# A four-layer graph network on one Trainium2 core: 36 sorted blocks instead of 32, 21 gathered blocks instead of 20, the sort's result through DRAM, gathers sent further ahead

## The chip, the cores and the metric

The kernel runs on one core of one Trainium2 chip. The metric is the time of the whole program on that core in microseconds (us), taken on the device. A profile comes from one execution of its own, which the hardware profiler recorded. The engines are called PE (matrix multiplication; PEld is its loading of weights), DVE (vectors), ACT (scalars and activations), POOL (general purpose, and here the engine that sends all DMAs with computed addresses) and SP (which sends plain DMAs).

## What is computed

N = 6250 nodes with C = 256 features, E = 100000 directed edges, four layers. The edges arrive sorted by destination, with random sources.

```python
def agg(h):
    return jax.ops.segment_sum(h[src], dst, num_segments=N)
x0 = x
x = jnp.maximum(_layernorm(x, axis=-1), 0.0)
for l in range(3):
    h = x + agg(x)
    h = jax.nn.relu(h @ W1s[l] + b1s[l])
    h = jax.nn.relu(h @ W2s[l] + b2s[l])
    x = h @ W3s[l] + b3s[l]
h = x + agg(x)
h = jax.nn.relu(h @ cW1 + cb1)
h = jax.nn.relu(h @ cW2 + cb2)          # cW2: 256 x 64, cW3: 64 x 256
return x0 + h @ cW3 + cb3
```

## The kernel before

**Blocks.** The nodes lie in NT = 49 blocks of 128 rows. The first 32 places (NS) are "s" blocks: all nodes of 32 row blocks are sorted by their number of incoming edges, and the s blocks hold them in that order, those with the fewest edges first. The other 17 (U) are "u" blocks, whose rows stay where they were. What a layer has computed for an s block is scattered row by row to the table in DRAM (`place_rows`: an indirect DMA that POOL sends, lines L598 and L600); u blocks are stored by SP as plain rows.

**Two ways to sum over the edges.** For most destination blocks PE does it. The features of all 49 row blocks lie on the chip in `XY`, as a high and a low part; for a *panel* of three or four destination blocks PE multiplies them with a matrix `a` of edge counts, 49 steps j of four matmuls each, 196 in a panel (`product`, L2087), summing into `agg`. A panel of four is 512 columns wide, one of three 384. The count matrices are stored as bytes in DRAM; SP loads them (`at<-mat`), ACT turns them into floats (L2052). For the s blocks with the fewest edges the sum is gathered instead (class `ByNode`): for the c-th edge of each of 128 nodes one indirect DMA, sent by POOL (L1761), brings 128 rows of the table; two at a time they are added by DVE into `sums` (L1798). A block whose nodes have at most 14 edges costs 14 such gathers. When a block is summed, PE turns it (`pt`, L1825), and it goes through the layer's dense part (`mlp`).

**A layer.** The panels come one after the other on PE; each closed panel goes through the dense part (L1567, L1570, L1666, L1671; in the last layer L1581, L1624, L1650) some steps later, in the midst of the next panel. The gathers run beside the panels. The last gathered block of a layer goes through a hastened form (`rush`, L1498 to L1533), and the last panel's own dense part follows at the start of the next layer. A layer's first gather may start only when every row of the table is written, since it may read any of them; PE may start the next layer at once with the u blocks, which stand first in `ORDER`, because they are kept on the chip. The s blocks come back from the table two at a time (`pairs_back`, tile `turned`), three such loads in flight.

**Layer 0** has more to do. The counts are not given: PE builds the matrices from one-hot vectors that DVE writes (L1234; PE L1288, ACT L1296), a little ahead of the panel that reads them. The sort by degree, its permutation of the nodes' words (generator `listed`, L1854 to L1870: one-hots on DVE, 32 small matmuls on PE) and the lists of addresses for the gathers also lie here: for each gathered block POOL fetches its nodes' edges (L1886, 20 requests ahead of the first gather), and 13 further requests bring the edges of the s blocks that PE sums.

**The order of the work.** Nothing is scheduled by a tool: the program is written step by step of PE's panels (`tick`), and every other engine's instruction is put into its queue at a step. `ByNode.flow` sends as many gathers at each step as a model of PE's time allows (`clock`, divided by `pace`, plus a lag from `LAGS`); `after` makes a gather wait until PE has come to the step. Eight tiles of two gathers each hold the rows on their way (`FIRST_TILES`, `MORE_TILES`). POOL works through its queue in order: a scatter that waits for its rows holds the gathers behind it.

Of the kernel before, what the change touches and what calls it, by code (L numbers as in the profile page):

```python
# [9 lines left out]
F32 = mybir.dt.float32  # L10
# [9 lines left out]
P = 128  # L20
# [400 lines left out]
def sorted_edges(  # L421
# [69 lines left out]
    NS = 32  # L491
# [3 lines left out]
    seq = [("u", b) for b in range(NS, NT - 3)] + [("s", b) for b in range(NS - 1, NS - 13, -1)] + [  # L495
        ("u", b) for b in range(NT - 3, NT)] + [("s", NS - 13)]
    early = [(0, 3)] + [(b, 4) for b in range(3, 23, 4)] + [(23, 3), (26, 3)]
    wide = [(b, 4) for b in range(0, 20, 4)] + [(20, 3), (23, 3), (26, 3)]
# [3 lines left out]
    nodes_of = [[(16, 4), (12, 4), (8, 4), (4, 4), (1, 3), (0, 1)]] * NLAYER + [  # L502
        [(15, 4), (11, 4), (7, 4), (3, 4), (1, 2), (0, 1)]]
# [34 lines left out]
    goal = const.tile([P, 2, NS], BF16, name="goal")  # L538
    V = 6
    what = const.tile([P, NS, V], BF16, name="what")  # L540
# [9 lines left out]
    tables = [dram.tile([N + PAD, C], F32, name=f"table{l}") for l in range(NLAYER + 1)]  # L550
    owns = [dram.tile([P * max(KS), C], F32, name=f"own{l}") for l in range(NLAYER + 1)]
# [43 lines left out]
    def place_rows(key, ap, b, sb, **kw):  # L595

        if placing[0]:
            nc.gpsimd.memset(mark, 0.0)  # L598
        placing[0] = True
        got = nc.gpsimd.indirect_dma_start(  # L600
            out=ap, out_offset=bass.IndirectOffsetOnAxis(ap=ids[:, b:b + 1], axis=0),
            in_=sb, in_offset=None, **kw)
        wrote(key, got, True)
# [291 lines left out]
    def ranking(pool):  # L895
# [5 lines left out]
        nc.gpsimd.tensor_copy(what[:, :, 0], place[:, 0:1].to_broadcast([P, NS]))  # L901
        nc.gpsimd.tensor_copy(what[:, :, 1], colf[:, :NS])
# [46 lines left out]
        nc.scalar.copy(what[:, :, 2], ps[:, :NS])  # L949
# [14 lines left out]
        at = pool.tile([P, NS], I32, name="at_i", bufs=1)  # L964
        nc.vector.tensor_tensor(at, ps[:, :NS], begins, OP.add)
# [35 lines left out]
        nc.vector.tensor_copy(goal, where)  # L1001
        bits = pool.tile([P, 3, NS], I32, name="bits", bufs=1)
        nc.vector.tensor_scalar(bits[:, 0], at, P - 1, None, op0=OP.bitwise_and)
        nc.vector.tensor_scalar(bits[:, 1], at, 7, None, op0=OP.arith_shift_right)
        nc.vector.tensor_scalar(bits[:, 2], at, 14, None, op0=OP.arith_shift_right)
# [1216 lines left out]
```

## Time and profile before

| | |
|---|---|
| median of 3 runs | 1986.4 us (1983.7 to 1999.28) |
| the profiled execution | 1992.96 us, its span 1991.1 us, so 1.9 us lie around the span |
| granted PE clock in it, mean | 0.966 |
| PE busy | 1853.7 us, 93% of the span |
| POOL busy | 1338.7 us, 67% |
| ACT / DVE busy | 1210.6 us, 61% / 915.1 us, 46% |
| start to layer 0's first panel | 153.3 us |
| layers 0, 1, 2, 3, by the first matmul of each | 522.6, 439.6, 438.1, 437.5 us |

The profile gives each engine's busy time, but a PE that is busy may run at a lower granted clock, and POOL's time between two requests, in which it prepares the next, isn't counted as busy. Rows of a group say: line, engine, operation, written tile <- read tiles, count | busy us, mean ns of one | idle us ahead of them, and which event ended that idle time. Rows of a timeline say: start, length, engine, line, operation, and in brackets the idle time ahead and what ended it.

### The profile page before, as it was taken

What the parts mean: (1) busy time and instruction counts of PE and PEld (TensorE: products, weight loads), DVE (VectorE), ACT (ScalarE), POOL (GpSimd) and SP (SyncE); (2) the same over time, 40 slices, a digit from 0 to 9 for tenths busy, and PEclk for the clock granted to TensorE, in tenths of its full rate; (3) what the DMA queues carried; (4) which work ended last, traced back from release to release, by engine and by line L of the source; (5) the groups of instructions that cost most, each with busy time, mean ns of one, the idle gap of its engine ahead of it and who ended that gap; (6) DMA issues with size and microseconds to landing.
All of it is one profiled execution on the core that took longest, in us unless ns stands there. A gap on an engine that the chain in (4) does not pass through costs nothing. (4 is left out here: it accounts for less than half of the span.)

```text
span 1991.1 us, 29317 instructions
## 1 busy us (share of the span) xinstructions
PE 1853.7 (93%) x9334; PEld 1483.0 (74%) x9334; DVE 915.1 (46%) x1915; ACT 1210.6 (61%) x2370; POOL 1338.7 (67%) x1496
## 2 busy tenths in 40 slices
PE   4868999999999899999999899999999899999896
PEld 3746666776788777777898777777898777777774
DVE  6789788676564243332333343333334353332232
ACT  3766666676666476566566376565665576665562
POOL 2521777777777566676777566677777567777775
PEclk9878999999999999999999899999999999999898
DMA  5523665666556485565566575555566676665663
GB/s 176 176 97 115 182 195 168 203 215 217 168 174 211 157 281 181 154 199 172 178 189 212 166 232 164 163 174 165 165 195 197 193 223 208 173 180 149 147 181 81
DMA packets 247119, 357.22 MB, mean 179 GB/s; under 512 B 33368, under 2 KB 201880, under 8 KB 246666
## 3 DMA queue, kind: packets, MB, share of 16 engines
q0 software_dynamic: 65584, 167.88, 29.2%
q1 hardware_dynamic: 179184, 184.72, 28.6%
q10 hardware_dynamic: 2186, 2.65, 0.4%
q8 instruction: 75, 1.23, 0.2%
q14 instruction: 90, 0.74, 0.1%
HBM read 289.20 MB, written 70.92 MB: 181 GB/s over the span
## 5 line engine op out<-in xcount | busy, mean ns | idle before, releaser
L2087 PE MATMUL agg<-a,XY 128*128 128x512 f32 (+1 forms) x6272 | 1471.4, 387 | 14.5 <-ACT a L2052 11.0
L1761 POOL DMA_INDIRECT rows<-table,idxN x1119 | 1076.6, 962 | 422.0 <-PE agg L2087 207.1
L2087 PEld LDWEIGHTS agg<-a,XY 128*128 128x128 f32 x6272 | 1150.1, 191 | 212.5 <-ACT a L2052 21.2
L2052 ACT CAST a<-at 128x512 fp32r<-128x512 uint8 (+1 forms) x1561 | 876.7, 585 | 328.6 <-PE agg L2087 317.9
L1798 DVE TENSOR_TENSOR sums<-sums,rows 128x512 f32<-128x512 f32 x471 | 328.5, 697 | 650.2 <-DMA rows<-table,idxN 627.0
L1296 ACT CAST at<-bp 128x392 uint16<-128x392 f32 x213 | 102.8, 488 | 119.9 <-PE bp L1288 115.8
L1567 PE MATMUL ps<-h,w 128*128 128x512 f32 (+1 forms) x312 | 132.5, 568 | 4.1 <-DVE zz L1671 3.1
L600 POOL DMA_INDIRECT table<-zz,ids x96 | 96.5, 1005 | 55.8 <-DVE zz L1533 23.0
L1666 PE MATMUL ps<-w,h 128*128 128x256 f32 x576 | 133.2, 384 | 0.0
L1666 PEld LDWEIGHTS ps<-w,h 128*128 128x128 f32 x576 | 110.8, 194 | 15.1
L1288 PE MATMUL bp<-hi,lo 128*128 128x98 bf16 x964 | 88.6, 219 | 32.5 <-DVE lo L1234 25.2
L1288 PEld LDWEIGHTS <-lo 128*128 128x128 bf16 x964 | 54.3, 103 | 86.1 <-DVE lo L1234 42.4
L1234 DVE TENSOR_TENSOR lo<-lanes,pairs 128x512 bf16<-128x512 bf16 x240 | 99.3, 423 | 31.4 <-PE bp L1288 30.1
L1567 PEld LDWEIGHTS ps<-h,w 128*128 128x128 f32 x312 | 60.0, 194 | 56.7 <-issue 38.4
L1671 DVE TENSOR_TENSOR zz<-ps,w 128x512 f32<-128x512 f32 x78 | 49.6, 647 | 103.2 <-PE ps L1666 102.1
L1570 ACT ACTIVATE h<-ps,bias 128x512 f32<-128x512 f32 (+1 forms) x78 | 49.8, 656 | 55.8 <-PE ps L1567 55.8
L1833 ACT ACTIVATE h<-pt,bias 128x256 f32<-128x256 f32 (+1 forms) x80 | 32.7, 460 | 83.3 <-PE pt L1825 83.3
L1234 DVE TENSOR_TENSOR hi<-hi,pairs 128x784 bf16<-128x784 bf16 x120 | 69.3, 578 | 4.2
L1234 DVE TENSOR_TENSOR hi<-cols,pairs 128x784 bf16<-128x784 bf16 x120 | 67.2, 560 | 0.6 <-ACT pairs L1222 0.6
L1886 POOL DMA_INDIRECT lane<-padded,at x20 | 20.3, 1016 | 65.5 <-PE bp L1288 59.7
L1392 DVE TENSOR_TENSOR XY<-turned,XY 128x512 fp32r<-128x512 f32 x48 | 32.7, 694 | 67.4 <-ACT XY L1391 67.3
L600 POOL DMA_INDIRECT out_dram<-zz,ids x32 | 50.8, 1588 | 15.2 <-issue 7.1
(261 smaller groups left out, 958.5 us busy)
## 6 DMA issues: line engine op xcount, KB each, us to landing
at<-mat SPq DMA_DIRECT2D x112, 448.0 KB
mat<-at SPq DMA_DIRECT2D x30, 784.0 KB
at<-mat SPq DMA_DIRECT2D x62, 336.0 KB
rows<-table,idxN POOLq DMA_INDIRECT x1119
turned<-table SPq DMA_DIRECT2D x48, 256.0 KB
at<-mat SPq DMA_DIRECT2D x50, 224.0 KB
at<-mat SPq DMA_DIRECT2D x84, 112.0 KB
own<-zz SPq DMA_DIRECT2D x59, 128.0 KB
```

What stands on the lines that cost most here:

```text
L600: got = nc.gpsimd.indirect_dma_start(out=ap, out_offset=bass.IndirectOffsetOnAxis(ap=ids[:, b:b + 1], axis=0), in_=sb, in_offset=None, **kw)
L1234: nc.vector.tensor_tensor(o, values, which[:, :, None, :].to_broadcast(shape), op)
L1288: mm = nc.tensor.matmul(bp[:, m * HW:(m + 1) * HW], lo[:, m, :], hi[:, m, :], start=(i == 0), stop=(i == len(sets) - 1))
L1296: nc.scalar.copy(o, v)
L1567: mm = nc.tensor.matmul(ps[:, :w], weights[l][0][:, c, i * P:(i + 1) * P], h1[:, c, :w], start=(c == 0), stop=(c == KC - 1))
L1570: later(soon, lambda: nc.scalar.activation(h2[0][:, i, :w], ps[:, :w], AF.Relu, bias=b2[l][:, i:i + 1]))
L1666: mm = nc.tensor.matmul(o, h2[0][:, c, nodes], w3[:, c, :], start=(c == 0), stop=(c == KC - 1))
L1671: later(soon, lambda: nc.vector.tensor_tensor(z[:, :m, :], v, w3[:, KC:, :].to_broadcast([P, m, C]), OP.add))
L1761: got = nc.gpsimd.indirect_dma_start(out=t[:, c % 2, :], out_offset=None, in_=tables[self.l][:, :], in_offset=bass.IndirectOffsetOnAxis(ap ...
L1798: nc.vector.tensor_tensor(sums, sums, rows.rearrange("p h c -> p (h c)"), OP.add)
L2052: nc.scalar.copy(o, v)
L2087: mm = nc.tensor.matmul(agg[c][:, :w], XY[:, j, o:o + P], a[:, :w], start=(i == 0 and half == 0), stop=(i == NT - 1 and half == 1))
```

## The change

All of it is on the same program; line numbers in the changed program are some 2 to 40 higher (a gather is L1791, a scatter L602, PE's panels L2116).

1. **Blocks.** NS 32 becomes 36, so 13 u blocks are left. 21 blocks are gathered in layers 0, 1, 2 (20 before), 19 in the last (as before). Counted over the lists, layer 0 sends 312 gathers (304), layers 1 and 2 send 291 each (284), the last 257 (267). The group that comes last is now the highest of the gathered blocks, block 20 (18 in the last layer), instead of block 0.
2. **Panels.** 28 blocks are summed by PE in layers 0 to 2 (29 before), 30 in the last (30). Layer 0: 3, 3, 3, 3, 4, 4, 4, 4 blocks (3, 4, 4, 4, 4, 4, 3, 3). Layers 1 and 2: seven panels of 4 (five of 4, three of 3). The last layer's widths stay.
3. **Sort.** The 32 matmuls and the one-hots of the permutation go. POOL scatters four words for each of 36 x 128 nodes to a table `ranks` in DRAM (36 requests), and one DMA reads it back as `got`. Of the list fetches, 8 come ahead of the first gather instead of 20; 13 more, and 17 requests for s blocks' edges instead of 13, lie among the gathers.
4. **Sending ahead.** Up to 3 (layer 0) or 5 gathers more may be sent at a step, if a tile is free. In the model, `SLOW` is 1.15 instead of 1, the lag of layers 1 to 3 is 11 instead of 12, and `AHEAD_OF` 9 instead of 4.
5. **Held scatters.** In layers 1 and 2 the scatters of the group (4, 4) and of the panel next to the last (s blocks 20 on) are put behind the layer's last gather in POOL's queue; their rows wait in tiles `xt`.
6. Small things: the u rows' own copies are loaded six blocks to a panel, the hastened chain's steps stand one step apart instead of two, `pairs_back` is called when the whole layer is stored.

```diff
-    NS = 32
+    NS = 36
-    early = [(0, 3)] + [(b, 4) for b in range(3, 23, 4)] + [(23, 3), (26, 3)]
-    wide = [(b, 4) for b in range(0, 20, 4)] + [(20, 3), (23, 3), (26, 3)]
+    early = [(b, 3) for b in range(0, 12, 3)] + [(b, 4) for b in range(12, 28, 4)]
+    wide = [(b, 4) for b in range(0, 28, 4)]
     final = [(b, 4) for b in range(4, 24, 4)] + [(24, 3), (27, 3), (0, 4)]
-    nodes_of = [[(16, 4), (12, 4), (8, 4), (4, 4), (1, 3), (0, 1)]] * NLAYER + [
-        [(15, 4), (11, 4), (7, 4), (3, 4), (1, 2), (0, 1)]]
+    nodes_of = [[(16, 4), (12, 4), (8, 4), (4, 4), (0, 4), (20, 1)]] * NLAYER + [
+        [(14, 4), (10, 4), (6, 4), (2, 4), (0, 2), (18, 1)]]
...
+        for g in range(NS):
+            place_rows("ranks", ranks[:, :], g, what[:, g, :], goal)
...
+            got = pool.tile([P, NS, 4], I32, name="got")
+            back = nc.gpsimd.dma_start(out=got, in_=ranks.rearrange("(p b) v -> p b v", p=P))
+            waits(back, [name for name, _ in written["ranks"]], "each node's words lie alone")
...
+            fetch_list(0)
+            fetch_list(1)
+            for _ in range(9):
+                yield
+            nc.vector.tensor_copy(ids, got[:, :, 0])
...
+            make_list(0)
...
-                if beside is not None and (p or i % 2):
+                if beside is not None and i % (3 if p else 2) == 0:
                     next(lists, None)
...
+        def holds(l, blocks):
+            if l in (0, NLAYER):
+                return False
+            b0, n = panels[l][-2]
+            return blocks in ([("s", nodes_of[l][-3][0] + i) for i in range(nodes_of[l][-3][1])],
+                              seq[b0:b0 + n])
...
-                    self.send(int((clock[0] - self.first + self.lag) / self.pace) + 1)
+                    self.send(int((clock[0] - self.first + self.lag) / self.pace) + 1 +
+                              MORE_AHEAD[self.l > 0], True)
...
+                        if early and taken[0] == FIRST_TILES + (late is not None) * MORE_TILES:
+                            return
...
+                    if self.sent == len(self.order):
+                        while held_rows:
+                            put(*held_rows.pop(0))
...
-        LAGS, CLOSE, AHEAD_OF, NEAREST, CLOSING = (9.0, 12.0), 2.0, 4.0, 5.0, 40.0
+        LAGS, CLOSE, AHEAD_OF, NEAREST, CLOSING = (9.0, 11.0), 2.0, 9.0, 5.0, 40.0
+        MORE_AHEAD = (3, 5)
```

On POOL, between the preparation of the features (`XY`) and the first gather of layer 0, the program before has this (the tile `lane` takes the fetched edges):

```order
L1093 TENSOR_TENSOR XY<-zs,XY 128x256
L1886 DMA lane<-padded,at 128x17 x4
L1886 DMA lane<-padded,at 128x16 x4
L1886 DMA lane<-padded,at 128x15 x4
L1886 DMA lane<-padded,at 128x14 x4
L1886 DMA lane<-padded,at 128x12 x3
L1886 DMA lane<-padded,at 128x10
L1761 DMA rows<-table_87,idxN 128x256 x16
```

and the changed program has, behind 34 more pairs of a scatter to `ranks` and a memset, this (the tile `run` takes the edges of gathered blocks, `edges` those of blocks that PE sums):

```order
L600 MEMSET mark 1x4
L602 DMA ranks<-what,goal 4608x4
L1887 DMA got<-ranks 128x144
L1893 DMA run<-padded,got 128x17 x4
L1893 DMA run<-padded,got 128x16 x4
L1791 DMA rows<-table_87,idxN 128x256 x13
L1893 DMA edges<-padded,got 128x63
L1791 DMA rows<-table_87,idxN 128x256
L1893 DMA run<-padded,got 128x14 x4
```

So 12 list fetches have moved behind the first gathers, and 36 scatters and a read stand ahead of them.

At the end of layer 1, POOL's queue before ends with a group's last four gathers and four scatters, the last of them that of the hastened block (table_88 is the layer's input, table_89 its result):

```order
L1761 DMA rows<-table_88,idxN 128x256 x4
L600 DMA table_89<-zz,ids 6378x256
L598 MEMSET mark 1x4
L600 DMA table_89<-zz,ids 6378x256
L598 MEMSET mark 1x4
L600 DMA table_89<-zz,ids 6378x256
L598 MEMSET mark 1x4
L600 DMA table_89<-zz,ids 6378x256
L1761 DMA rows<-table_89,idxN 128x256 x106
```

In the changed program 48 gathers stand ahead of 13 scatters, eight of them from `xt`; this piece begins with the last of the eight:

```order
L602 DMA table_89<-xt,ids 6378x256
L600 MEMSET mark 1x4
L602 DMA table_89<-zz,ids 6378x256
L600 MEMSET mark 1x4
L602 DMA table_89<-zz,ids 6378x256
L600 MEMSET mark 1x4
L602 DMA table_89<-zz,ids 6378x256
L600 MEMSET mark 1x4
L602 DMA table_89<-zz,ids 6378x256
L600 MEMSET mark 1x4
L602 DMA table_89<-zz,ids 6378x256
L1791 DMA rows<-table_89,idxN 128x256 x117
```

On PE at that place, the program before turns the last gathered block one step (four matmuls) after the next layer has begun; the rows begin with the dense part of a gathered group, and L1567 is the last panel's own:

```order
L1666 MATMUL ps<-w_8249,h_11874 128x256 x6
L2087 MATMUL agg<-a,XY 128x384 x12
L1567 MATMUL ps<-h_11943,w_8247 128x384 x4
L2087 MATMUL agg<-a,XY 128x512 x4
L1498 MATMUL pt<-ident,u 128x128 x2
L2087 MATMUL agg<-a,XY 128x512 x4
L1514 MATMUL ps<-h1s,w_8247 128x128 x4
L1666 MATMUL ps<-w_8249,h_11948 128x256 x6
L2087 MATMUL agg<-a,XY 128x512 x4
L1527 MATMUL ps<-w_8249,h1s 128x256 x2
L2087 MATMUL agg<-a,XY 128x512 x184
```

and the changed program turns it two steps ahead of the end of the layer's last panel:

```order
L1691 MATMUL ps<-w_8304,h_11581 128x256 x8
L2116 MATMUL agg<-a,XY 128x512 x20
L1522 MATMUL pt<-ident,u 128x128 x2
L2116 MATMUL agg<-a,XY 128x512 x4
L1538 MATMUL ps<-h1s,w_8302 128x128 x4
L2116 MATMUL agg<-a,XY 128x512 x4
L1551 MATMUL ps<-w_8304,h1s 128x256 x2
L1592 MATMUL ps<-h_11692,w_8302 128x512 x4
L2116 MATMUL agg<-a,XY 128x512 x4
L1691 MATMUL ps<-w_8304,h_11697 128x256 x8
L2116 MATMUL agg<-a,XY 128x512 x176
```

So the block's chain (turn, second and third product) has moved from the start of the next layer to the end of this one, and the last panel's own dense part, four blocks wide now, is what is left behind the boundary.

More of the change, by code (lines that the diff above doesn't have):

```diff
@@ L1360, in step @@
             g["steps"].pop(0)()
-            free[0] = now[0] + (2 if g["hurry"] else 4)
+            free[0] = now[0] + (1 if g["hurry"] else 4)
             if g["steps"]:
@@ L1489, in store @@
             if stored[l] == NT:
+                assert placed[l] == NS and not held_rows
+                pairs_back(l)
                 layers[l + 1].begin()
@@ L1726, in ready @@
                     return False
-                if self.l == NLAYER and now[0] >= ends[self.l] - 2:
+                if now[0] >= ends[self.l] - (2 if self.l == NLAYER else 0):
                     return True
@@ L1950, in listed @@
                     yield
+                if j % 3 == 0:
+                    fetch_list(2 + j // 3)
+                    if j and 1 + j // 3 < len(lists):
+                        make_list(1 + j // 3)
                 if j < HELD:
@@ L2065, in product @@
                 ask_first()
-            if l == 1 and p < NS // 4:
-                for b in range(4 * p, 4 * p + 4, 2):
-                    later(12 + 6 * (b % 4), lambda b=b: own_rows(b, b + 2))
+            if l == 1:
+                for i, b in enumerate(range(6 * p, min(6 * p + 6, NS), 2)):
+                    later(10 + 12 * i, lambda b=b: own_rows(b, b + 2))
             agg = [ps_a.tile([P, W], F32, name="agg") for _ in range(KC)]
```

173 lines of the change are left out of this document (81 added, 92 removed).

## The prediction

> **What bounds the kernel now.** First the page: busy shares, then the span in slices.
>
> ```profile
> span 1991.1 us, 29317 instructions
> PE 1853.7 (93%) x9334; PEld 1483.0 (74%) x9334; DVE 915.1 (46%) x1915; ACT 1210.6 (61%) x2370; POOL 1338.7 (67%) x1496
> PE   4868999999999899999999899999999899999896
> POOL 2521777777777566676777566677777567777775
> ```
>
> PE is full nearly everywhere; POOL never reaches 8 tenths, and looks far from a bound. That reading needs the stages: start, layers 0 to 3.
>
> ```profile
> 0.00:153.30 153.30, 102.30 (x664) 78.60 (x665) 110.94 (x310) 87.27 (x208) 54.28 (x104) 0.85 0.47 151
> 153.30:675.90 522.60, 495.86 (x3000) 377.15 (x3001) 358.85 (x866) 341.02 (x727) 365.28 (x388) 0.98 0.59 184
> 675.90:1115.50 439.60, 428.00 (x1918) 352.11 (x1917) 149.06 (x248) 266.15 (x493) 304.81 (x338) 0.99 0.61 191
> 1115.50:1553.60 438.10, 428.54 (x1919) 353.95 (x1917) 149.69 (x248) 263.75 (x488) 303.46 (x340) 0.98 0.59 180
> 1553.60:1991.10 437.50, 399.03 (x1840) 321.18 (x1838) 146.60 (x244) 252.47 (x458) 310.83 (x329) 0.95 0.60 171
> ```
>
> Columns: window; its length; busy us of PE, PEld, DVE, ACT, POOL; granted clock, DMA share, GB/s. PE idles 26.7 us in layer 0, 11.6 and 9.6 in layers 1 and 2, 38.5 in the last with its tail. Removing matmuls can give about what PE is busy with, provided that POOL delivers as early. So POOL's own groups, in a stretch late in layer 1 and one late in the last layer:
>
> ```profile
> L1761 POOL DMA_INDIRECT rows<-table,idxN x102 | 97.2, 953 | 32.2 <-PE agg L2087 13.9 <-issue 10.4 <-PE ps L1666 1.8
> L600 POOL DMA_INDIRECT table<-zz,ids x20 | 19.8, 992 | 4.9 <-issue 3.7 <-DVE sums L1794 0.6 <-DVE sums L1798 0.5
> L598 POOL MEMSET mark<- 1x4 f32 x14 | 1.3, 92 | 0.0
> ...
> L1761 POOL DMA_INDIRECT rows<-table,idxN x161 | 153.1, 951 | 49.1 <-PE agg L2087 20.4 <-issue 20.4 <-DVE sums L1798 3.3
> L600 POOL DMA_INDIRECT out_dram<-zz,ids x21 | 33.4, 1592 | 5.9 <-issue 4.7 <-DVE sums L1798 0.6 <-DMA rows<-table,idxN 0.6
> ```
>
> The first stretch is 960 to 1114 us: busy 118.3, idle 37.1, together all of it. The idle time is 0.3 us per request, whoever is named as its releaser: a gather occupies POOL (97.2+32.2)/102 = 1.27 us, a scatter with its memset 1.30 to 1.33; in the last layer 1.256 and (33.4+5.9)/21 = 1.87, with its memset's 8.6/21 on top at most 2.28. **POOL is saturated there at "7 tenths".** So each layer is a cycle: a gather stream, the last block's chain, the table's last write, the next layer's first gather. Its joints, in the timeline:
>
> ```profile
> 673.22 0.95 POOL L1761 DMA_INDIRECT rows<-table,ids  x1 [0.30 <-PE agg L2087]
> 680.75 0.44 PE L1498 MATMUL pt<-ident,u 128*128 128x128 f32 x2 [3.45 <-DVE u L1816]
> 693.39 0.98 POOL L1761 DMA_INDIRECT rows<-table,idxN  x1 [2.24 <-PE agg L2087]
> 1113.82 0.95 POOL L1761 DMA_INDIRECT rows<-table,idxN  x1 [0.30 <-issue]
> 1119.71 0.69 PE L1498 MATMUL pt<-ident,u 128*128 128x128 f32 x2 [2.79 <-DVE u L1812]
> 1129.94 1.17 POOL L600 DMA_INDIRECT table<-zz,ids  x1 [11.19 <-DVE zz L1533]
> 1133.54 0.97 POOL L1761 DMA_INDIRECT rows<-table,idxN  x1 [2.42 <-PE agg L2087]
> ```
>
> From one layer's `pt` to the next is 1119.71 - 680.75 = 438.96 us, first gather to last 420.4. At saturated prices 284 gathers and 28 scatters take 284x1.27 + 28x1.32 = 398. So POOL had some 22 us of slack, held back early in the layer by the pacing, and PE (428 busy) is the tighter of the two by a little. I work with both clocks and take the later.
>
> **Layers 1 and 2.** What PE saves: a panel of four and a panel of three, their 196 matmuls alone:
>
> ```profile
> 1176.60:1229.70 53.10, 46.91 (x196) 36.79 (x197) 1.00 0.57 172
> 1012.50:1052.80 40.30, 35.94 (x199) 34.65 (x198) 1.00 0.68 209
> ```
>
> Three panels of 3 become two of 4: 3x35.94 - 2x46.91 = 14.0 less; the whole panels, with what else PE does in them, give 3x40.3 - 2x53.1 = 14.7, of which one block's dense part only moves to another place. I take 12: PE's 428 becomes 416. The boundary's idle 10 us shrinks to about 4, since `pt` now stands ahead of the panel's end and its wait is filled by the panel: PE's clock says 420.
>
> POOL's clock: 291x1.26 + 23 scatters among them x1.33 = 397 for the stream. Behind it come last gather to `pt`, 5.9 (1113.82 to 1119.71), and `pt` to first gather, 13.8 before. The moved chain is the same; the 13 scatters behind the last gather take 13x1.33 = 17.3, beside the 16.1 from last gather to the hastened scatter (1129.94). I put `pt` to first gather at 18, since the 4-wide last panel stores its u rows later. 397 + 5.9 + 18 = 421, and 4 for tiles that aren't free: **425**. POOL is the later one. 438.96 - 425 = 14 a layer, with a range of 5 (the slack stays) to 20 (PE's clock and less): **-27 for both**.
>
> That the eight held scatters cost nothing rests on the chain of the last block: POOL stood idle for 11.19 us before the scatter at 1129.94. Without that cover each would cost 1.33, 10.6 in all. Held behind them are that chain's own scatter and the next layer's first gather, nothing else. In exchange the gathers in front of them come 10.6 us earlier.
>
> **The sort.** What goes on DVE and PE, and POOL's start:
>
> ```profile
> L1863 DVE TENSOR_TENSOR moved<-block,what 128x768 bf16<-128x768 bf16 x8 | 7.7, 958 | 0.3
> L1854 DVE TENSOR_TENSOR lane<-lanes,goal 128x512 bf16<-128x512 bf16 x8 | 5.5, 683 | 0.0
> L1858 DVE TENSOR_TENSOR block<-lanes,goal 128x128 bf16<-128x128 bf16 x8 | 2.3, 282 | 0.0
> 123.87 3.81 POOL L1093 TENSOR_TENSOR XY<-zs,XY 128x512 fp32r<-128x512 f32 x3 [1.71 <-ACT XY L1088]
> 187.40 0.98 POOL L1886 DMA_INDIRECT lane<-padded,at  x1 [59.72 <-PE bp L1288]
> L1886 POOL DMA_INDIRECT lane<-padded,at x20 | 20.3, 1016 | 65.5 <-PE bp L1288 59.7 <-issue 5.2 <-DVE lo L1234 0.3
> 213.81 0.94 POOL L1761 DMA_INDIRECT rows<-table,idxN  x1 [0.30 <-issue]
> 155.00:205.00 50.00, 43.35 (x330) 36.14 (x328) 47.23 (x110) 32.11 (x78) 13.64 (x14) 0.95 0.36 112
> ```
>
> DVE loses 15.5 us of work in a stretch in which it is full (47.23 of 50). POOL is free at 127.7 and stood 59.7 us waiting. In that hole go 36 scatters. No 16-byte scatter is in the trace. The nearest rows are L600's (992 plus gap and memset, 1.33) and the fetches (1.016 + 0.3); ends: 1.2 and 2.3 (the last layer's scatter). I take 1.33: 48 us, to 175. Landing 2.4 (from the wait ahead of 1133.54), the read 1 plus some 3 (last gather to `pt`, 5.9, less the sum): **the first list fetch at about 181.5** against 187.4. DVE's copy of `got` stands at step 20 of panel 0, some 173 to 177 at 1.0 to 1.2 us a step (59.1 us for its 49 before, a panel of 3 in both programs), and the first list's arithmetic seven steps on needs edges that land near 188; so DVE and then PE stall some 10 us there in all, which eats most of the 15.5.
>
> The Trainium skill, "DMA: Bandwidth & Descriptors", section "SWDGE vs HWDGE vs iDMA", says that POOL writes its requests' descriptors into on-chip memory from which DVE's two-port mode locks it out. That speaks against 36 scatters in DVE's fullest stretch. In the row above, fetches beside a full DVE took 1016 ns against 953 for gathers beside a light one, so by the trace the rule is worth 6%, some 3 us of the 48, which changes the sum by less than its range. Taken at its worst, with POOL shut out for as long as DVE is busy, the scatters would not be done before 200 and the page's rule would make the sum about nothing.
>
> **Layer 0** has 30 list and edge fetches more among its gathers (8 ahead). Its stream in the trace and its price late in the layer (560 to 674 us):
>
> ```profile
> L1761 POOL DMA_INDIRECT rows<-table,idxN x67 | 65.2, 973 | 22.2 <-issue 11.3 <-PE agg L2087 5.3 <-DVE lo L1234 1.2
> ```
>
> A gather takes 87.4/67 = 1.305. Before: 33 fetches, 304 gathers and 28 scatters from 187.40 to 674.17 are 486.8 for 365 requests, 1.334 each. After: 38 + 312 + 31 = 381 requests. At 1.334 they end at 181.5 + 508 = 690; at saturated prices (38x1.32 + 312x1.305 + 31x1.33 = 498) at 680; at layer 1's 1.26 a gather at 665. PE saves 11 us of a panel and part of its 26.7 idle and would reach that place at 650 to 663. POOL is the later: I take 680 against 674.2, and count **+7** with the longer chain behind it; range -9 to +15.
>
> **Last layer.** Its joints:
>
> ```profile
> 1557.88 0.44 PE L1498 MATMUL pt<-ident,u 128*128 128x128 f32 x2 [2.93 <-DVE u L1812]
> 1570.58 0.97 POOL L1761 DMA_INDIRECT rows<-table,idxN  x1 [2.26 <-PE agg L2087]
> 1960.92 0.95 POOL L1761 DMA_INDIRECT rows<-table,idxN  x1 [0.30 <-issue]
> ```
>
> Same panels, 257 gathers (-10) and 29 scatters among them (25 before): -12.6 + 4x1.87 = -5; but the first gather comes at `pt` + 18, against 12.7 here. The stream had slack in its first part, which sending five ahead uses. The tail of 30 us behind the last gather has the same instructions. **-5**, range -12 to +3.
>
> **Sum:** +7 - 27 - 5 = -25. The profiled execution took 1992.96, so it would take 1968; the median of the runs lies 6.6 lower, at 1986.4, and from that I forecast **1961**. The DMA engines (0.59 to 0.61 busy) carry 12 gathers more and 392 fewer matmuls' weights; they don't bind.
>
> **Rivals.** (a) *POOL keeps up everywhere.* Then PE's savings all count: layer 0 ends at 655 instead of 676 (-20), layers 1 and 2 -19 each, and the last layer loses some of its idle time near the end (-2): -60, **1926**. For it: POOL's 22 us of slack per layer, the five ahead. Against it: saturation in each layer's last 150 us, and 38 + 312 + 31 requests in layer 0. (b) *POOL takes all that PE gives.* Eight tiles can limit the stream, since DVE waits for rows all the time, up to 9.5 us:
>
> ```profile
> DVE sums L1798 <- DMA rows<-table,idxN: 627.0, 273, 9.5
> ```
>
> If so the early slack can't be used: layers 1 and 2 cost 438 again and layer 0 is 15 longer, the last -5, the boundaries -8: about **1988**, no change. (c) *Slower: the scatters to `ranks`.* Each word's row is 16 bytes, 128 rows a request, and all 36 must have landed. If one occupies POOL for 2.6 us or more, 36x1.3 = 47 us more: lists from 228 instead of 181, layer 0's stream, which POOL bounds, moves by that, +54, and with -32 from the rest **2008**. It decides from about 2.3 us per scatter. Against it: the scatters of 1-KB rows take 1.33. (d) *PE's clock.* In the last layer a stretch with idle PE was granted less:
>
> ```profile
> 1858.20:1913.20 55.00, 44.48 (x227) 41.60 (x226) 14.33 (x24) 27.43 (x56) 43.01 (x46) 0.84 0.65 167
> ```
>
> If PE waits for POOL at each layer's end in pieces as there (10.5 us idle, clock 0.84), each costs some 7 us more than the wait itself (44.48 busy x 0.16): three of them make 1961 into **1982**. The Trainium skill, "TensorE: Matmul & The Clock Gate", Part 1, says that an idle window of some 3.4 us halves the clock. The row above agrees in kind; by the rule alone the waits of under 3 us ahead of `pt` cost nothing extra.
>
> **How the numbers follow.** Forecast (1945 to 1972): 0.45. (a), with cases between it and the forecast: 0.19. (b): 0.14. (d): 0.11. (c): 0.08. That the sort's part doesn't do what it says has 0.03: its DVE stall could grow to the whole 20 us of a late `got`, which ends in (b). About 1% is what a measurement here can tell from no change: faster is below 1966.5. From the forecast 0.37 of 0.45 and all of (a) lie there, with 0.02 of the others: 0.58. Same, to 2006.3: 0.33. Slower: 0.09. The range leaves out the far end of (a) and (c): 1928 to 1992.
>
> **What will show it.** Right: PE's panel matmuls 5880 instead of 6272; `pt` to `pt` in layers 1 and 2 near 425, with POOL without gaps over 0.4 us from the first gather to the last; layer 0's last gather near 680, and its first list fetch near 181; DVE idle some 10 us before the copy of `got`. Wrong: `pt` to `pt` at 415 or less (PE binds, a), or at 435 (tiles bind, b); `ranks` scatters at over 2 us (c); granted clock under 0.9 in the panels around the boundaries (d). What I trust least is layer 0, where a tenth of a microsecond per request moves the end by 38 us, and the first gathers' time behind the boundary.

## The result, and the profile after

The changed kernel takes 1968.92 us (median of 4 runs, 1966.87 to 1971.6), the kernel before 1990.1 us in the same comparison (four runs, 1983.7 to 1999.28). The ratio is 0.9891, with a 95% interval of 0.9846 to 0.9936: about 1% faster. On one other chip, where both programs run 11 to 15% longer, the same change was 3% slower; that is in the experiments (e0).

The page of the changed kernel, busy shares and slices:

```profile
span 1969.3 us, 28333 instructions
PE 1810.7 (92%) x8984; PEld 1411.1 (72%) x8984; DVE 907.0 (46%) x1899; ACT 1174.8 (60%) x2256; POOL 1419.5 (72%) x1625
POOL 2567777777777757677777777677777776777775
```

POOL's row is where the change shows: its digits stand at 7 nearly throughout, where before there were 5s and 6s in the first half of each layer. The stages, by the first panel matmul of each layer (window; length; busy us of PE, PEld, DVE, ACT, POOL; clock, DMA share, GB/s):

```profile
0.00:154.49 154.49, 100.96 (x685) 76.39 (x685) 112.65 (x305) 86.83 (x208) 77.14 (x144) 0.89 0.48 150
154.49:695.37 540.88, 491.94 (x3044) 382.31 (x3045) 348.71 (x865) 333.78 (x726) 408.00 (x449) 0.95 0.58 180
695.37:1119.79 424.42, 413.18 (x1717) 318.21 (x1715) 152.40 (x248) 251.01 (x436) 310.66 (x348) 1.00 0.63 197
1119.79:1542.34 422.55, 412.27 (x1716) 318.54 (x1715) 152.57 (x248) 249.67 (x432) 315.17 (x357) 1.00 0.61 187
1542.34:1969.30 426.96, 392.33 (x1830) 315.64 (x1828) 140.64 (x234) 253.49 (x457) 308.52 (x329) 0.96 0.62 172
```

Against before: start +1.2, layer 0 +18.3, layers 1 and 2 -15.2 and -15.6, the last -10.5, in all -21.8. These borders are not the same place in both programs, since the last block's chain moved ahead of the border. The joints are: POOL's first scatter of the sort, its first list fetch, last gather of layer 0, first and last gather of layer 1, first of layer 2, first and last of the last layer; and PE's three `pt`:

```profile
128.98 1.02 POOL L602 DMA_INDIRECT ranks<-what,goal  x1 [0.17 <-issue]
182.95 1.20 POOL L1893 DMA_INDIRECT run<-padded,got  x1 [2.27 <-DMA got<-ranks]
678.82 0.95 POOL L1791 DMA_INDIRECT rows<-table,ids  x1 [0.30 <-issue]
705.66 0.98 POOL L1791 DMA_INDIRECT rows<-table,idxN  x1 [11.45 <-DMA table<-zz]
1107.94 0.95 POOL L1791 DMA_INDIRECT rows<-table,idxN  x1 [0.30 <-PE agg L2116]
1128.61 0.98 POOL L1791 DMA_INDIRECT rows<-table,idxN  x1 [3.15 <-PE agg L2116]
1551.30 0.98 POOL L1791 DMA_INDIRECT rows<-table,idxN  x1 [3.16 <-PE agg L2116]
1937.87 0.94 POOL L1791 DMA_INDIRECT rows<-table,idxN  x1 [0.30 <-issue]
...
687.05 0.69 PE L1522 MATMUL pt<-ident,u 128*128 128x128 f32 x2 [4.88 <-DVE u L1850]
1112.86 0.44 PE L1522 MATMUL pt<-ident,u 128*128 128x128 f32 x2 [1.55 <-DVE u L1846]
1535.41 0.44 PE L1522 MATMUL pt<-ident,u 128*128 128x128 f32 x2 [1.45 <-DVE u L1846]
```

Start to first `pt`: 687.05 against 680.75, +6.3. `pt` to `pt`: 425.81 and 422.55 against 438.96 and 438.17, -13.2 and -15.6. Last `pt` to the end: 433.9 against 433.2, +0.7. These four make up the -21.8. Why layers 1 and 2 are shorter is in POOL's groups from layer 1's first gather to its last, before and after:

```profile
L1761 POOL DMA_INDIRECT rows<-table,idxN x284 | 271.7, 957 | 115.7 <-PE agg L2087 72.6 <-issue 21.3 <-PE ps L1666 7.8
...
L1791 POOL DMA_INDIRECT rows<-table,idxN x291 | 277.8, 955 | 107.4 <-PE agg L2116 39.2 <-issue 37.2 <-DMA table<-zz 11.4
```

The idle time in these rows fell from 115.7 to 107.4 us, and the after row has 11.4 us ahead of the first gather in it (2.2 before), so within the stream 113.5 became 96.0. (The names of the releasers say less: the 33 us that went from "PE agg" came back by half as "issue".) POOL's gaps above the usual 0.3 us, summed over the timeline from layer 1's first gather to its last, are 27.9 us before and 7.9 after. Among the gathers lie 23 scatters instead of 28, some 6.5 us less, and seven gathers more, some 8.8 us more: the stream takes 402.3 us instead of 420.4. In layer 0, from the first list fetch to the last gather, these gaps fell from 14.1 to 0.2 us: there POOL has no slack left at all.

### The profile page after: what moved, and what is told of

It is laid out like the page before. It is cut to its first block, busy times and chain, and to the rows that moved or that the text cites. A ratio compares the mean times of both kernels' runs of the same rounds, so it can differ in the third digit from the quotient of the medians.

```text
span 1969.3 us, 28333 instructions
## 1 busy us (share of the span) xinstructions
PE 1810.7 (92%) x8984; PEld 1411.1 (72%) x8984; DVE 907.0 (46%) x1899; ACT 1174.8 (60%) x2256; POOL 1419.5 (72%) x1625
## 5 line engine op out<-in xcount | busy, mean ns | idle before, releaser
L2116 PE MATMUL agg<-a,XY 128*128 128x512 f32 (+1 forms) x5880 | 1424.8, 395 | 14.5 <-ACT a L2080 11.0
L1791 POOL DMA_INDIRECT rows<-table,idxN x1130 | 1091.4, 966 | 385.4 <-PE agg L2116 148.6
L2116 PEld LDWEIGHTS agg<-a,XY 128*128 128x128 f32 x5880 | 1084.9, 191 | 234.7 <-ACT a L2080 23.6
L2080 ACT CAST a<-at 128x512 fp32r<-128x512 uint8 (+1 forms) x1463 | 839.7, 600 | 325.9 <-PE agg L2116 322.8
L602 POOL DMA_INDIRECT table<-zz,ids x92 | 90.7, 986 | 29.8 <-issue 17.2
L1592 PEld LDWEIGHTS ps<-h,w 128*128 128x128 f32 x296 | 56.0, 190 | 53.6 <-issue 44.3
L1697 DVE TENSOR_TENSOR zz<-ps,w 128x512 f32<-128x512 f32 x66 | 43.1, 672 | 106.1 <-PE ps L1691 106.0
L602 POOL DMA_INDIRECT out_dram<-zz,ids x36 | 57.2, 1589 | 15.4 <-issue 9.1
L1828 DVE COPY sums<-rows 128x512 f32<-128x512 f32 x61 | 42.3, 694 | 54.8 <-DMA rows<-table,idxN 53.8
L1393 DVE TENSOR_TENSOR XY<-turned,XY 128x512 fp32r<-128x512 f32 x54 | 37.0, 693 | 63.0 <-ACT XY L1397 62.8
```

Of the source, the lines that this page charges most:

```text
L602: got = nc.gpsimd.indirect_dma_start(out=ap, out_offset=bass.IndirectOffsetOnAxis(ap=at[:, b:b + 1], axis=0), in_=sb, in_offset=None, **kw)
L1592: mm = nc.tensor.matmul(ps[:, :w], weights[l][0][:, c, i * P:(i + 1) * P], h1[:, c, :w], start=(c == 0), stop=(c == KC - 1))
L1697: later(soon, lambda: nc.vector.tensor_tensor(z[:, :m, :], v, w3[:, KC:, :].to_broadcast([P, m, C]), OP.add))
L1791: got = nc.gpsimd.indirect_dma_start(out=t[:, c % 2, :], out_offset=None, in_=tables[self.l][:, :], in_offset=bass.IndirectOffsetOnAxis(ap ...
L2080: nc.scalar.copy(o, v)
L2116: mm = nc.tensor.matmul(agg[c][:, :w], XY[:, j, o:o + P], a[:, :w], start=(i == 0 and half == 0), stop=(i == NT - 1 and half == 1))
```

## The experiments

Two theories were set against each other. P: POOL's stream of requests sets the length of layers 0 to 2, and the gain comes from a stream with fewer gaps. M: PE sets it, and the gain comes from 392 fewer matmuls. Each experiment edits the changed kernel; times are medians, ratios are against the kernel before, timed beside it on the same chip. The changed kernel itself (ratio 0.9891) was not timed on the chips of e4 to e11, so differences from it in microseconds go across chips; the ratios give them within some 2 us.

**e4: less work for PE.** In layers 1 and 2, 16 of a panel's 196 matmuls are left out.

```diff
                     for half in range(2):
+                        if half and l in (1, 2) and i % 6 == 3:
+                            continue
```

> The changed kernel, leaving out 16 of a panel's 196 matmuls in layers 1 and 2 (the low part at 8 of the 49 steps, so those sums are a little less exact): 28 us less PE work a layer, POOL's requests unchanged. Theory P: POOL ends the layer where it did, 0 to 3 less a layer: 1963 to 1969. Theory M: 25 to 28 less a layer, 1913 to 1920.

1954.48 us, ratio 0.9818 (0.9794 to 0.9842), some 14 less than the changed kernel. Layer 1's first and second `pt`, and POOL's gathers in between:

```profile
685.77 0.44 PE L1522 MATMUL pt<-ident,u 128*128 128x128 f32 x2 [3.92 <-DVE u L1850]
1105.69 0.44 PE L1522 MATMUL pt<-ident,u 128*128 128x128 f32 x2 [2.39 <-DVE u L1846]
...
L1791 POOL DMA_INDIRECT rows<-table,idxN x291 | 277.6, 954 | 101.5 <-PE agg L2118 42.1 <-issue 39.9 <-DVE sums L1832 4.9
```

The layer is 419.92 from `pt` to `pt`, 5.9 shorter, while PE's busy time between these two fell by 22.7 us (414.6 to 391.9); layer 2 is 3.5 shorter for 18.4. So P holds for most of what PE was spared; the rest counted, against an expectation of 0 to 3, and the time fell below P's 1963 to 1969. Of POOL's idle time, 101.5 us, 11.3 lie ahead of the first gather: what is left is 0.31 for each of the others, hardly more than the 0.3 that always stands between two requests (0.33 in the changed kernel). The stream is 396.6 us long. The 5.7 us more of the changed kernel went with the PE work, so they were waits for PE's steps.

**e5: the sort's scatters sent twice.**

```diff
-        for g in range(NS):
+        for g in list(range(NS)) * 2:
```

> The changed kernel, with each of the 36 scatters to the sort's table sent twice (the same words to the same rows). Theory P: 36 x 1.31 = 47 us more before the lists, layer 0's stream of requests is saturated from there on and ends 47 later: 2016 (2010 to 2020). Theory M: PE sets layer 0, the stream catches up, PE only stalls in the first panel: 1980 to 1995.

2010.6 us, ratio 1.0105 (1.0074 to 1.0135). First list fetch and last gather of layer 0:

```profile
229.77 1.20 POOL L1893 DMA_INDIRECT run<-padded,got  x1 [2.36 <-DMA got<-ranks]
724.49 0.95 POOL L1791 DMA_INDIRECT rows<-table,ids  x1 [0.31 <-issue]
```

46.8 later at the front, 45.7 later at the layer's last gather, 42 in the time: layer 0 is POOL's from the lists on, and what stands ahead of them counts nearly one to one. This run also shows what a busy neighbour costs a scatter: first the stretch beside a busy DVE (127 to 175 us, DVE busy 41.1 of 48), then the one beside an idle DVE (175 to 226, 0.8 of 51):

```profile
L602 POOL DMA_INDIRECT ranks<-what,goal x33 | 35.6, 1079 | 7.0 <-issue 7.0
L602 POOL DMA_INDIRECT ranks<-what,goal x40 | 38.6, 966 | 8.7 <-issue 8.7
```

The same kind of scatter takes 1079 ns in the first and 966 in the second. PE and ACT were idle too in the second stretch, so the run doesn't tell which of the three costs it.

**e6: the sort's permutation on DVE and PE as before**, the rest of the change kept but for two small things: some of the sort's tiles have one buffer instead of two, and the s blocks' edges are asked for a little sooner.

```diff
-        for g in range(NS):
-            place_rows("ranks", ranks[:, :], g, what[:, g, :], goal)
...
+                for g in range(G4):
+                    nc.tensor.matmul(sums[:, :V * NS], lane[:, g],
+                                     moved[:, g].rearrange("p v b -> p (v b)"),
+                                     start=(g1 + g == 0), stop=(g1 + g == NS - 1))
```

> The changed kernel with the sort's permutation of before: nine groups of one-hots on DVE and 36 matmuls on PE instead of 36 scatters and a read (with one buffer instead of two for its tiles, and the edges of the s blocks asked for a little sooner). Theory P: the first list fetch comes some 6 us later than 183, the stream with it, and DVE has 17 us more in its full stretch: layer 0 +6 to +12, 1975 to 1981. If instead the way through DRAM is what made layer 0 18 us longer: 1955 to 1962.

1980.21 us, ratio 0.9956 (0.9939 to 0.9973): 11 more than the changed kernel.

```profile
194.32 1.31 POOL L1927 DMA_INDIRECT lane<-padded,at  x1 [64.83 <-issue]
687.62 0.95 POOL L1795 DMA_INDIRECT rows<-table,ids  x1 [0.30 <-issue]
```

The lists start 11.4 later and the layer's last gather comes 8.8 later. The way through DRAM is worth about 10 us, and the two rows show where: POOL's request stream starts earlier, and e5 has shown that a later start counts. Whether sparing DVE and PE is worth anything beyond that was not separated.

**e7: scatters held in layer 0 too**, with four gather tiles there instead of seven, so that the rows find room.

```diff
-            if l in (0, NLAYER):
+            if l == NLAYER:
...
-        FIRST_TILES, MORE_TILES, PAIRS = 7, 1, 3
+        FIRST_TILES, MORE_TILES, PAIRS = 4, 4, 3
```

> The changed kernel, with the eight scatters held back in layer 0 too (four of the eight gather tiles are given up in layer 0 for the rows that wait). Theory P: layer 0's last gather 10 us earlier; PE waited 8.3 and 4.9 us for gathered blocks in the layer's last panel, and these go: 8 less (4 to 10), 1961, unless four tiles are too few for the stream, then longer than 1969 by up to 15. Theory M: 1969.

1963.33 us, ratio 0.9861 (0.9836 to 0.9886).

```profile
672.56 0.95 POOL L1790 DMA_INDIRECT rows<-table,ids  x1 [0.30 <-PE agg L2115]
680.85 0.69 PE L1522 MATMUL pt<-ident,u 128*128 128x128 f32 x2 [3.95 <-DVE u L1849]
```

The last gather comes 6.3 earlier, `pt` 6.2, the time is 5.6 less. It is not the 10 of eight scatters: with four tiles the stream has nine gaps that are 7.3 us longer in all than the usual 0.3, where it had none; but a gather took 0.987 us on the mean instead of 1.001. As expected by P, though the two intervals overlap and the runs were on different chips; the trace carries the verdict.

**e8: nothing sent further ahead.**

```diff
-        MORE_AHEAD = (3, 5)
+        MORE_AHEAD = (0, 0)
```

> The changed kernel with no gather sent further ahead (3 and 5 become 0), on another chip than the first time. Theory P (POOL's stream sets layers 0 to 2; sending ahead is what lets it run without gaps): the early slack comes back, layers 1 and 2 some 15 longer each, layers 0 and 3 some 5 each: about 2005 (1990 to 2012). Theory M (fewer matmuls on PE bring the gain): 1969.

1988.38 us, ratio 0.9977 (0.996 to 0.9994): 19 more than the changed kernel, half of what was expected, and just below P's range of 1990 to 2012.

```profile
L1791 POOL DMA_INDIRECT rows<-table,idxN x291 | 276.6, 950 | 112.5 <-PE agg L2116 59.1 <-issue 32.6 <-DVE sums L1832 5.6
693.18 0.69 PE L1522 MATMUL pt<-ident,u 128*128 128x128 f32 x2 [6.43 <-DVE u L1850]
1123.30 0.44 PE L1522 MATMUL pt<-ident,u 128*128 128x128 f32 x2 [1.49 <-DVE u L1846]
```

The first `pt` is 6.1 later, layer 1 is 430.1 (4.3 more), not 441: layer 1's stream takes 406 us, not 420. Its gaps above 0.3 us are 13.1 us in all, against 7.9 in the changed kernel and 27.9 before. So sending ahead takes up 5 us of the 20; the rest lies with other parts of the change. The numbers of the pacing (the lag, `AHEAD_OF`, `SLOW`) were not tried apart; the block numbers are a part of it, as e9 will show.

**e9: the block numbers of before**, all else of the change kept.

```diff
-    NS = 36
+    NS = 32
...
-    early = [(b, 3) for b in range(0, 12, 3)] + [(b, 4) for b in range(12, 28, 4)]
-    wide = [(b, 4) for b in range(0, 28, 4)]
+    early = [(0, 3)] + [(b, 4) for b in range(3, 23, 4)] + [(23, 3), (26, 3)]
+    wide = [(b, 4) for b in range(0, 20, 4)] + [(20, 3), (23, 3), (26, 3)]
...
+    nodes_of = [[(16, 4), (12, 4), (8, 4), (4, 4), (1, 3), (0, 1)]] * NLAYER + [
+        [(15, 4), (11, 4), (7, 4), (3, 4), (1, 2), (0, 1)]]
```

> The changed kernel with the numbers of blocks of before (32 sorted, 20 gathered, panels as before), on another chip than the first time. Theory P: layers 1 and 2 turn to PE's clock, +8 each; layer 0 has 365 requests instead of 381 and loses its 13 us of PE waiting for gathered blocks, -15 to -20; the last layer +2: about 1969 (1960 to 1982). Theory M: 14 a layer in layers 1 and 2 and 5 in layer 0 are lost: 2000 (1993 to 2008).

**1946.77 us, ratio 0.978 (0.9755 to 0.9805): the fastest of all, 22 less than the changed kernel.** The four layers, then first list fetch, last gather of layer 0 and its `pt`:

```profile
151.32:667.83 516.51, 494.65 (x2983) 377.14 (x2983) 346.53 (x836) 340.18 (x729) 385.75 (x420) 0.98 0.60 188
667.83:1093.70 425.87, 420.99 (x1918) 347.36 (x1917) 150.22 (x248) 266.92 (x494) 304.29 (x341) 1.00 0.63 197
1093.70:1516.32 422.62, 420.69 (x1919) 347.53 (x1917) 150.07 (x248) 263.82 (x488) 305.26 (x342) 1.00 0.61 187
1516.32:1942.90 426.58, 388.73 (x1826) 312.29 (x1824) 143.45 (x237) 251.84 (x455) 307.97 (x322) 0.97 0.61 174
...
176.61 1.18 POOL L1893 DMA_INDIRECT run<-padded,got  x1 [2.28 <-DMA got<-ranks]
654.73 0.97 POOL L1791 DMA_INDIRECT rows<-table,ids  x1 [0.30 <-PE agg L2116]
659.01 0.44 PE L1522 MATMUL pt<-ident,u 128*128 128x128 f32 x2 [3.21 <-DVE u L1850]
```

Layers 1 to 3 take 425.9, 422.6 and 426.6 us, the changed kernel's 424.4, 422.6 and 427.0: 28 blocks or 29 on PE, 291 gathers or 284, the length is the same. With 29 blocks PE has 5 and 2 us of idle time a layer and binds, and POOL's gaps in layer 1's stream are 19.2 us above the usual 0.3; with 28 PE has 11 and 10 us, the gaps are 7.9, and POOL is the later. Layer 0 is another matter: its last gather comes 24.1 earlier, of which 6.3 stand ahead of the first list fetch (four scatters fewer at 1.34 make 5.4) and 17.8 come from 365 requests instead of 381. Theory M, which would have lost 31 us here, is out. P's own forecast of 1969 missed too, by 22 us. It had put +8 on each of layers 1 and 2 for PE, and from `pt` to `pt` they took 0.8 and 0.1 more: PE was busy for 421 us there, not for the 428 of before that the forecast used. And layer 0 gave 28 (`pt` at 659.01 instead of 687.05) where 15 to 20 were expected.

**e10: no scatters held.**

```diff
-            if l in (0, NLAYER):
+            if l >= 0:
                 return False
```

> The changed kernel with no scatters held back in layers 1 and 2, on another chip than the first time. Theory P: the last gather 8 x 1.27 = 10 us later, the joint behind it 2 shorter (no scatters queue there): +8 a layer, 1985 (1980 to 1990). Theory M: 1969 to 1972.

1991.23 us, ratio 1.0001 (0.9982 to 1.002): 22 more.

```profile
1119.15 0.69 PE L1522 MATMUL pt<-ident,u 128*128 128x128 f32 x2 [9.09 <-DVE u L1846]
1553.63 0.69 PE L1522 MATMUL pt<-ident,u 128*128 128x128 f32 x2 [8.56 <-DVE u L1846]
```

Layer 1 takes 435.6 us from `pt` to `pt` and layer 2 434.5, 9.8 and 11.9 more than with the held scatters, and PE waits 9.09 and 8.56 instead of 1.55 and 1.45: without the cover the eight scatters cost their 10 us a layer in full, and a little more in layer 2, where 8 were expected (the time lies just above the range of 1980 to 1990). Layer 1's stream is 10.1 us longer, and from the next `pt` to the first gather it is 17.8 us instead of 15.75: 2 are lost there that were to be gained.

**e11: one block less gathered in the last layer**, one more on PE, with seven gather tiles instead of eight.

```diff
-        [(14, 4), (10, 4), (6, 4), (2, 4), (0, 2), (18, 1)]]
+        [(13, 4), (9, 4), (5, 4), (1, 4), (0, 1), (17, 1)]]
```

> The changed kernel, with 18 blocks gathered in the last layer instead of 19 and 31 summed by PE instead of 30 (and seven gather tiles instead of eight): 241 gathers instead of 257, 12 us more for PE there, and one more block of counts to build in layer 0. Theory P: POOL's stream in the last layer 16 x 1.256 = 20 us shorter, PE has 427 - 392 = 35 of idle time there of which 16 wait for gathered blocks, so PE ends it: 8 to 12 less; layer 0 +1 to +3: 1961 (1956 to 1968). Theory M: PE's 12 us more count in full, and layer 0's 6: 1981 to 1987.

1963.74 us, ratio 0.9858 (0.9821 to 0.9895). From the last `pt` to the end, this kernel and the changed one:

```profile
1540.90:1960.30 419.40, 403.58 (x1853) 316.89 (x1851) 135.31 (x224) 262.83 (x464) 298.62 (x324) 0.99 0.63 174
...
1535.41:1969.30 433.89, 399.26 (x1858) 320.44 (x1858) 141.77 (x237) 257.71 (x465) 314.15 (x341) 0.97 0.62 172
```

14.5 less in the last layer, with more PE work; 5.5 of it is lost ahead, where layer 2's `pt` comes at 1540.90 instead of 1535.41. Layer 0's `pt`, behind the block more that is built there, comes only 0.2 later (687.30); the other 5.2 come in layers 1 and 2, whose work is the same but for the seven tiles, so these are the likely cause. So in the last layer too the gathers were one block too many.

**e0 to e3: the changed kernel and three of these edits on another chip.** e0 is the changed kernel itself; e1, e2 and e3 have the edits of e8, e10 and e9.

> The changed kernel once more, on the chip of the next three, so that they are compared with it and not only with the kernel before: 1969 us, the same within 0.3%, by every theory.

> The changed kernel, with no gather sent further ahead (3 and 5 become 0). Theory P (POOL's stream of requests sets the length of layers 0 to 2, and the change gains because it uses the stream's early slack of some 20 us): the slack comes back, layers 1 and 2 some 15 longer each, layers 0 and 3 some 5 each, in all about 2005 (1990 to 2012). Theory M (the 392 matmuls less bring the gain, PE sets the length): 1969, no change.

> The changed kernel, with no scatters held back: the eight of layers 1 and 2 go among the gathers. Theory P: the last gather comes 8 x 1.27 = 10 us later, and what is gained behind it is 2, so each of the two layers is 8 longer: 1985 (1980 to 1990). Theory M: PE has work meanwhile and POOL time to spare, 1969 to 1972.

> The changed kernel with the numbers of blocks of before: 32 sorted, 20 gathered, panels as before; the sort through DRAM, the sending ahead and the held scatters stay. Theory P: in layers 1 and 2 PE becomes the later clock, 428 busy and some 4 of waiting, +8 each; layer 0 has 365 requests instead of 381, and POOL would be done 27 earlier, so PE ends it, some 15 to 20 earlier; the last layer +2: about 1969, the block numbers give nothing in sum (1960 to 1982). Theory M: the gain of 14 a layer in layers 1 and 2 goes, and 5 of layer 0: 2000 (1993 to 2008).

Here the kernel before took 2201.16 us, the changed one 2268.49 (ratio 1.0307, 1.0275 to 1.0339), e1 2266.24 (1.0294), e2 2269.18 (1.0288), e3 2224.78 (1.0099, 1.0069 to 1.0129). On the chips of e4 to e11 the kernel before took 1988 to 1993 us, so this chip is the exception. The expectations in microseconds are void, e0's first of all, but the order tells something. PE's waits, and POOL's gathers in layer 1 of e0:

```profile
PE agg L2116 <- issue: 100.8, 126, 5.1
...
904.39 0.94 POOL L1791 DMA_INDIRECT rows<-table,idxN  x1 [1.83 <-PE agg L2116]
...
914.78 0.94 POOL L1791 DMA_INDIRECT rows<-table,idxN  x1 [1.94 <-PE agg L2116]
923.86 0.94 POOL L1791 DMA_INDIRECT rows<-table,idxN  x1 [1.89 <-PE agg L2116]
```

A gather itself takes what it took (0.94), but in these rows every seventh or eighth comes 1.5 to 1.6 us late. In layer 1 of e0, 41 of 291 gathers stood over 0.6 us idle, in the first profile of this kernel 7, and the stream took 461.4 us (818.60 to 1280.03) instead of 402.3: the late ones are the whole difference. So a request of POOL costs on the mean a seventh more there (461.4/402.3). PE has stalls too for which the profile names no cause ("issue", 100.8 us; none of them in the first profile). And in all four profiles from this chip waits of POOL, ACT and DVE end by a releaser called "remote" (before POOL's gathers in e0: 39 waits, 70.2 us), which none of the other profiles has.

With the block numbers of before (e3) the kernel is 44 us faster than e0, 33 of them ahead of the first `pt` (767.04 against 800.43): layer 0's requests count here too, and more. Sending ahead (e1) and holding (e2) move nothing. Without the held scatters layer 1's stream is 10 us longer here as well (471.6), but the time doesn't show it. All this but e2, which P would have slower, fits theory P with a dearer POOL; it is no test of P, since all these engines stall there. What causes the stalls stays open, and with it why the change as a whole loses 3% on this chip.

## Why the prediction was right

It said 1961 us, a change of -25.4; measured were 1968.92 and -21.2. Half of the miss in the time is the start: the median before is 1990.1 over four runs where the forecast began at 1986.4. So its own border for "faster", 1966.5, was missed too. The profiles differ by 21.8, and by its steps:

- **The sort, start of layer 0.** First list fetch at about 181.5: it came at 182.95. A scatter was priced at 1.33:

```profile
L602 POOL DMA_INDIRECT ranks<-what,goal x36 | 37.6, 1045 | 7.6 <-issue 7.6
L600 POOL MEMSET mark<- 1x4 f32 x35 | 3.3, 94 | 0.0
...
182.20 0.19 DVE L1927 COPY ids<-got 128x36 int32<-128x36 int32 x1 [8.75 <-DMA got<-ranks]
```

  48.5 us for 36 are 1.35 each. DVE stood 8.75 us before the copy and 3.1 more before the first list's arithmetic, where 10 in all were expected. Rival (c) is out; 16 bytes a row cost hardly more than 1 KB (1045 ns against 977 for the scatters of layer 1). In the Trainium skill, "DMA: Bandwidth & Descriptors", "SWDGE vs HWDGE vs iDMA", DVE can lock POOL out of the descriptors' memory. e5 agrees in kind, and is the cleaner measure: 1079 ns beside a DVE that is busy for 41 of 48 us, 966 beside an idle one, 12% or 4 us for 36 scatters, where the prediction put 3; that it is this lock isn't shown.
- **Layer 0.** +7 with the last gather near 680: +6.3 and 678.82. 381 requests took 495.9 us from the first list fetch, 1.30 each; 498 were expected. PE waited for POOL there: its idle time grew from 26.7 to 48.9 us, and the granted clock fell from 0.98 to 0.95.
- **Layers 1 and 2.** 425 each: 425.8 and 422.6. That settles rivals (a), 415 or less, and (b), 435; and the granted clock was 1.00 in both layers, so (d) is out there. The stream was put at 397 and 4 for tiles that aren't free; it took 402.3. The sign "no gaps over 0.4 us" was not met: 18 of layer 1's requests behind the first have one. They aren't the tiles': in e4, with the same tiles and less work for PE, two are left and the stream takes 396.6, the sum's 397. `pt` to first gather was put at 18; it is 15.75 and 15.89 in layers 2 and 3, with the 13 scatters ending at 1125.46 and then their landing, and 18.6 only behind layer 0, where it waits for the u rows.
- **Last layer: this step failed.** -5 was expected, +0.7 came. The stream itself did what the sum said: 386.6 us instead of 390.3, with ten gathers fewer and four scatters more. The price of such a scatter, 1.87, was right. All of them, then two near the end with the memset between them:

```profile
L602 POOL DMA_INDIRECT out_dram<-zz,ids x29 | 46.1, 1591 | 8.0 <-issue 7.7 <-DVE sums L1832 0.3
...
1931.45 1.62 POOL L602 DMA_INDIRECT out_dram<-zz,ids  x1 [0.30 <-issue]
1932.49 0.62 POOL L600 MEMSET mark<- 1x4 f32 x1
1933.38 1.59 POOL L602 DMA_INDIRECT out_dram<-zz,ids  x1 [0.27 <-issue]
```

  From the one scatter to the next is 1.93 us; from scatter to next request the mean of all 29 is 1.90, as it was before. The memset is recorded inside the scatter's own time (it begins at 1932.49, the scatter ends at 1933.07), so it is not to be added on top, as the prediction's bound of 2.28 had it. What failed is the joint. The prediction knew that the first gather would come later behind `pt` and let the slack in the stream's first part take that up, by sending five ahead. The gather came 3.2 later (15.89 instead of 12.70), and the slack was not used: POOL's gaps above 0.3 us are 8.0 us in that stream before and 9.4 after. And the tail, put as unchanged, is 1.2 longer. -3.8, +3.2 and +1.2 are the +0.7.
- **What the sum hid.** The forecast put layers 1 and 2 down to fewer matmuls and the use of POOL's slack together. The experiments take them apart. From `pt` to `pt` the two layers became 13.2 and 15.6 us shorter. Undoing the held scatters (e10) gives back 9.8 and 11.9 of that, sending nothing ahead (e8) 4.3 and 4.8, the block numbers (e9) 0.8 and 0.1: the first two alone make up the gain. The new block numbers give nothing in layers 1 to 3 and cost layer 0 its 28 us (`pt` at 659.01 or at 687.05). The prediction knew that layer 0 would grow by its requests and that POOL was the later clock in layers 1 and 2, and did not add the two up against the block numbers. Its own numbers for PE with all the matmuls are 428 us and 4 at the border, 432; e9 measured 421.0 and 4.9, so the gain of layers 1 and 2 was to be had without leaving any out. Apart from the last layer the steps had the right size, +7, -27 and -5 against +6.3, -28.8 and +0.7, so the time is no luck. But the new block numbers, which come first in the change, were a loss, and the sum did not show it.

Undone one at a time, by medians: held scatters 22 us, sending ahead 19, sort through DRAM 11, block numbers -22 (by the ratios 22, 17, 13, -22). They sum to 30 where the whole change gives 21; the parts feed the same stream, and how they overlap was not measured.

## What to carry to other kernels

An engine at "7 tenths" may be saturated: divide a stretch's busy and idle time by its instructions, and see whether the idle part is a fixed gap (0.3 us here). Here two engines were nearly level, and taking work from one to the other gave nothing in the balanced stages and was paid in the stage where the receiver was already late (layer 0); a count of requests per stage, times their price, would have shown it before a run. An ordering was worth more than any work removed: eight scatters put behind the last gather gave 10 us a layer. And a change should be tried part by part even when its sum comes out: one part of this one cost as much as the best part gave.

## What the runs showed of the hardware

PE after a wait: the four panel matmuls behind the first and the second `pt` (start, length, count), whose own rows, with the waits of 4.88 and 1.55 us ahead of them, stand in the result; then those behind the second `pt` of the kernel before, which waited for 2.79 us:

```profile
687.39 2.06 PE L2116 MATMUL agg<-a,XY 128*128 128x512 f32 x4
1113.05 1.19 PE L2116 MATMUL agg<-a,XY 128*128 128x512 f32 x4
...
1120.05 2.06 PE L2087 MATMUL agg<-a,XY 128*128 128x512 f32 x4
```

After 4.88 us of idle time four matmuls took 2.06 us, after 1.55 they took 1.19. The Trainium skill, "TensorE: Matmul & The Clock Gate", Part 1, has PE at half rate after an idle window of some 3.4 us, watched by a free-running window. The first two rows agree. Before the change a wait of 3.45 us (680.75) was followed by 1.19, as a window that began elsewhere would have it; but the one of 2.79 was followed by 2.06, and no idle window of 3.4 us has room in it. So the length of one wait doesn't decide it here, and the prediction's sentence that waits under 3 us cost nothing by that rule has a counterexample among its own rows (1119.71).

A scatter that adds to what lies in DRAM (`out_dram`) holds POOL for 1591 ns, one that overwrites (layer 1) for 977. From such a scatter's start to that of the next request it is 1.90 us on the mean, against 1.31 for the overwriting ones of layer 1: 0.6 us more.
